# The score banks of a linear attention as one unit with fixed readers, and a one-column product ahead of its four products

## The chip, the cores and the metric

The kernel runs on one core of a Trainium2 chip. The metric is the device time of one execution in microseconds (us). For the kernel before there are three runs: 2646.0, 2646.59 and 2646.84 us, median 2646.59.

## The reference, cut to what matters

The reference is a stack of four transformer-like layers on an activation of 4 sequences of 1024 positions and 128 features, all fp32. Each layer normalises, runs an attention-like part, adds it with a gate, normalises again and runs a feed-forward part. The change lies in the attention part of the second layer ("layer 1"), which is itself a small transformer of 4 inner layers with 16 heads of 8 features and causal linear attention in chunks of 128 positions:

```python
KV = jnp.einsum('bnchd,bnche->bnhde', k, v)
KVcum = jnp.cumsum(KV, axis=1) - KV
inter = jnp.einsum('bnchd,bnhde->bnche', q, KVcum)
den_inter = jnp.einsum('bnchd,bnhd->bnch', q, Kcum)
scores = jnp.einsum('bnchd,bnkhd->bnhck', q, k)
mask = jnp.tril(jnp.ones((CHUNK, CHUNK), dtype=bool))
scores = jnp.where(mask, scores, 0.0)
intra = jnp.einsum('bnhck,bnkhe->bnche', scores, v)
out = (inter + intra) / (den_inter + den_intra + ATT_EPS)[..., None]
```

After each attention comes an output product, a layer norm, a feed-forward part with Gelu, and another layer norm. The change concerns `scores` and the causal mask on them.

## The kernel before, in words

The activation lies feature-major in SBUF, 128 partitions by 4 x 1024 columns. A *step* n (0 to 7) is one chunk of 128 positions of all four sequences, so 512 columns. Layer 1's attention (`l1_attn`) has 4 inner layers of 8 steps, 32 steps in all, and in each of them 4 *batches* b, one a sequence: 128 batches.

The order of the work is made in two places. The kernel has a planner of its own, `Flow`: each strand of the work is a generator that asks for buffers (`take`, `one`), tells the planner what it costs an engine (`run(PE=...)`), and marks what it has done. The planner picks the strand that can start first by its own clock, the lower rank first, and so fixes the order in which the program is written. Buffers are kept in stocks by kind; those that came free first are handed out first (`sort` by `free_at`). When the program is built, a scheduler below may still move single instructions of an engine past each other where their data allow it. On the chip each engine then works through its own queue in that order and waits on semaphores.

PSUM has eight banks. In this part three are for general use ("ps"), one holds the attention's numerator ("acc"), and four are for scores ("sp", line 850).

For each batch the strands do this:

- `scores` (lines 981 to 994) takes the four score banks and writes them by four products, d = 2, 3, 1, 0. Product d uses 32 of the 128 partitions (rows 32d to 32d+31 of TensorE's array): the keys of that row group as weights (32x128) and the queries of four heads as 512 columns. All products are recorded by the helper `mm` (line 291). An fp32 product shows as two records (two passes) in the trace.
- `mask_dve` (996 to 1008) multiplies the scores of d = 0, 1, 2 with the causal mask into SBUF tiles "at" on VectorE, line 1005.
- `mask_act` (1010 to 1023) copies the scores of d = 3 into SBUF on ScalarE (line 1018), and GpSimd multiplies them with the mask there (line 1021).
- `values` (1055 to 1086) multiplies the masked scores with the values (line 1080) into "acc", 16 small products a batch, 32 output rows each.

Around them, `prep` makes queries, keys, values and denominators of a step up to three steps ahead (Exp on ScalarE, line 895), `state` sums the running KV, `attn_out` closes a step, and `tail` runs the output norm and the feed-forward part (Gelu on ScalarE, line 1127) up to one step behind. Exp and Gelu lie in different function tables of ScalarE, so a change between them puts an ACT_TABLE_LOAD before the instruction.

In the kernel before, the four banks are four buffers of the stock "sp". Their order in the stock follows from when they came free, so the bank that ScalarE read for one batch becomes bank 0 of the next, and the banks of d = 0, 1, 2 become those of 1, 2, 3. In the built program VectorE masks d = 2 first, then 1, then 0.

Of the kernel before, what the change touches and what calls it, by code (L numbers as in the profile page):

```python
# [12 lines left out]
ALU = mybir.AluOpType  # L13
# [97 lines left out]
class Flow:  # L111
# [43 lines left out]
    def run(self, chains):  # L155
        live = [{"gen": g, "t": 0.0, "want": None, "rank": 0.0, "no": i} for i, g in enumerate(chains)]
        while live:
            ready, asked = [], set()
            for c in sorted(live, key=lambda c: (c["rank"], c["no"])):
                if c["want"] is not None and c["want"][0] == "take":  # L160
                    kind = c["want"][1][0]
                    if kind in asked:
                        continue
                    asked.add(kind)
                s = self._start(c)
                if s is not None:
                    ready.append((s, c))
            assert ready, [c["want"] for c in live]
            first = min(s for s, _ in ready)
            at, c = next((s, c) for s, c in ready if s <= first + self.SLACK)  # L170
            got = None
            if c["want"] is None or c["want"][0] == "rank":
                self.at = c["t"]
            elif c["want"][0] == "spawn":
                self.at = c["t"]
                live.append({"gen": c["want"][1], "t": c["t"], "want": None, "rank": c["rank"], "no": c["no"]})
            elif c["want"][0] == "run":
                end = c["t"]
                table, costs = c["want"][1]
                if table and table != self.table:  # L180
                    self.table = table
                    self.clock["ACT"] += self.TABLE
                for e, cost in costs.items():
                    self.clock[e] = max(self.clock[e], c["t"]) + cost
                    end = max(end, self.clock[e])
                c["t"] = self.at = end + self.LATENCY
            elif c["want"][0] == "wait":
                c["t"] = self.at = at
            else:
                kind, n = c["want"][1]  # L190
                self.free[kind].sort(key=lambda b: b.free_at)
                got = [self.free[kind].pop(0) for _ in range(n)]
                c["t"] = self.at = at
            try:
                c["want"] = c["gen"].send(got)
                if c["want"][0] == "rank":
                    c["rank"] = c["want"][1]
            except StopIteration:
                live.remove(c)
# [6 lines left out]
def take(kind, n=1):  # L206
    return ("take", (kind, n))


def one(kind):  # L210
    (b,) = yield take(kind)
    return b


def rank(r):

    return ("rank", r)
# [7 lines left out]
def wait(key):  # L225
    return ("wait", key)


def mm_len(n, m=P):

    return max(n, m) * 0.00167 + 0.01


def dve_len(n):
    return 0.16 + 0.00104 * n


def act_len(n):
    return 0.25 + 0.00083 * n


def pool_len(n):
    return 0.2 + 0.0021 * n
# [6 lines left out]
def adaln_stack_kernel(ctx: ExitStack, tc: tile.TileContext, a):  # L250
    nc = tc.nc
    V, S, G, PE = nc.vector, nc.scalar, nc.gpsimd, nc.tensor
# [37 lines left out]
    def mm(out, lhsT, rhs, start=True, stop=True):  # L290
        PE.matmul(out, lhsT, rhs, start=start, stop=stop)  # L291

    def rep(ap, n):

        return ap.unsqueeze(1).to_broadcast([ap.shape[0], n, ap.shape[1]])
# [5 lines left out]
    def v4(t):  # L301
        return t.rearrange("p (a b) -> p a b", b=P)
# [11 lines left out]
    def K(name):  # L314
        lo, hi = _CONST[name]
        return cst[:, lo:hi]
# [9 lines left out]
    ident, mu, sl = K("ident"), K("mu"), K("sl")  # L326
# [148 lines left out]
    def flow():  # L475
        return Flow()

    def banks():
        return [ps() for _ in range(6)] + [acc() for _ in range(2)]
# [4 lines left out]
    def norm_stock(fl, n):  # L484

        fl.stock("xt", [v4(norm_tile(("ln_xc", "ln_sq", "ln_xn")[i % 3])) for i in range(n)])
        for kind, shape in (("st", (P, 4, 6)), ("mv", (P, 4, 2)), ("ve", (P, 4)), ("rs", (P, 4))):
            stock(fl, kind, 2, shape)
# [352 lines left out]
    def l1_attn():  # L841
        y4 = h4
        fl = flow()
# [3 lines left out]
        psum = banks()  # L847
        fl.stock("ps", psum[:3])
        fl.stock("acc", psum[3:4])
        fl.stock("sp", psum[4:])  # L850
        norm_stock(fl, 3)
        fl.stock("z", [v4(norm_tile(tag)) for tag in ("ln_xc", "ln_sq", "ln_xn")])
        stock(fl, "qx", 2, (P, 4, B, P))
# [124 lines left out]
        ats, nums = {}, {}  # L978
        every = [(l, n) for l in range(L1L) for n in range(NS)]

        def scores():

            for l, n in every:
                yield rank(l * NS + n)
                yield wait(("prep", l, n))
                k, qx = ready[l, n][1].t, ready[l, n][5].t
                for b in range(B):
                    sps = yield take("sp", 4)
                    yield run(PE=mm_len(512) + 0.2)
                    for d in (2, 3, 1, 0):  # L990
                        g = slice(32 * d, 32 * d + 32)
                        mm(v4(sps[d].t), k[g, b, :], qx[g, :, b, :])
                    ats[l, n, b] = [sps, None, None]
                    fl.mark(("scores", l, n, b))

        def mask_dve():
            for l, n in every:
                yield rank(l * NS + n)
                for b in range(B):
                    yield wait(("scores", l, n, b))  # L1000
                    sps = ats[l, n, b][0]
                    at3 = yield take("at", 3)
                    yield run(DVE=3 * dve_len(512))
                    for d in range(3):
                        V.tensor_tensor(at3[d].t, v4(sps[d].t), rep(mu, 4), ALU.mult)  # L1005
                    fl.give(*sps[:3])
                    ats[l, n, b][1] = at3
                    fl.mark(("dve", l, n, b))

        def mask_act():  # L1010
            for l, n in every:
                yield rank(l * NS + n)
                for b in range(B):
                    yield wait(("scores", l, n, b))
                    sp = ats[l, n, b][0][3]
                    a = yield from one("at")
                    yield run(ACT=act_len(512))
                    S.copy(a.t, v4(sp.t))  # L1018
                    fl.give(sp)
                    yield run(POOL=pool_len(512))  # L1020
                    G.tensor_tensor(a.t, a.t, rep(mu, 4), ALU.mult)  # L1021
                    ats[l, n, b][2] = a
                    fl.mark(("act", l, n, b))
# [92 lines left out]
        def tail_step(l, n, z):  # L1116
# [22 lines left out]
            if l == L1L - 1:  # L1139
# [4 lines left out]
                fl.give(o)  # L1144

        chains = [attn_out(), state(), values(), mask_dve(), mask_act(), scores()]
        fl.run(chains + [tail(0), tail(1), prep(0), prep(1), first()])

# [699 lines left out]
    for i, half in enumerate([l0, l1_attn, l1_ffn, l2_attn, l2_ffn, l3_attn, l3_ffn]):  # L1848
        if half is l1_attn:
            early.close()  # L1850
        if half is l2_attn:
            late.close()
        with tc.tile_pool(name=f"half{i}", bufs=2) as wk:
            half()
# [99 lines left out]
```

## Time and profile before

One execution was profiled. It took 2641.42 us in all, with a span of 2639.7 us from its first to its last instruction, at a mean granted TensorE clock of 0.929.

| | us | share of the span |
|---|---|---|
| profiled execution | 2641.42 | |
| its span | 2639.7 | |
| TensorE busy | 2308.3 | 87% |
| TensorE weight loads | 1387.7 | 53% |
| VectorE busy | 1333.0 | 50% |
| ScalarE busy | 1154.9 | 44% |
| GpSimd busy | 892.2 | 34% |
| layer 1's attention, by its lines | about 370 to 1540 | 44% |

"PE" is TensorE's products, "PEld" its weight loads, which overlap them; DVE is VectorE, ACT ScalarE, POOL GpSimd. A group line names the line of the kernel, the engine, the operation, the tile written and the tiles read, then the number of records, the busy time in us (the union of the records), the mean of one in ns, and the engine's idle time just before them with what ended it. A line of the timeline has the start in us, how long the merged records lasted, the engine, the group and the number of records merged. A line of the windows view has the stretch and, for each engine, its busy time and number of records, then the clock and DMA figures.

### The profile page before, as it was taken

What the parts mean: (1) busy time and instruction counts of PE and PEld (TensorE: products, weight loads), DVE (VectorE), ACT (ScalarE), POOL (GpSimd) and SP (SyncE); (2) the same over time, 40 slices, a digit from 0 to 9 for tenths busy, and PEclk for the clock granted to TensorE, in tenths of its full rate; (3) what the DMA queues carried; (4) which work ended last, traced back from release to release, by engine and by line L of the source; (5) the groups of instructions that cost most, each with busy time, mean ns of one, the idle gap of its engine ahead of it and who ended that gap; (6) DMA issues with size and microseconds to landing.
All of it is one profiled execution on the core that took longest, in us unless ns stands there. A gap on an engine that the chain in (4) does not pass through costs nothing.

```text
span 2639.7 us, 36709 instructions
## 1 busy us (share of the span) xinstructions
PE 2308.3 (87%) x13822; PEld 1387.7 (53%) x13822; DVE 1333.0 (50%) x3930; ACT 1154.9 (44%) x1964; POOL 892.2 (34%) x885
## 2 busy tenths in 40 slices
PE   5999989899999988889899869999799878788966
PEld 4654445454545444444454434444789633687842
DVE  5764346664654556655665554343654224455422
ACT  3653245445545444444444333333544226545424
POOL 1334444332433333333333222333634001544400
PEclk9999989998999989999999888999899879899978
DMA  5323300000000000000000001110000000000001
GB/s 209 88 67 99 101 0 1 1 1 1 1 1 1 1 1 1 1 1 1 1 1 1 1 33 64 65 65 33 1 1 1 1 26 7 1 1 1 1 1 48
DMA packets 29010, 61.46 MB, mean 23 GB/s; under 512 B 4256, under 2 KB 4512, under 8 KB 27808
## 3 DMA queue, kind: packets, MB, share of 16 engines
q1 hardware_dynamic: 27072, 53.86, 6.3%
q0 software_dynamic: 896, 3.16, 0.4%
q8 instruction: 109, 1.79, 0.3%
q10 hardware_dynamic: 864, 2.09, 0.2%
q14 instruction: 69, 0.57, 0.1%
HBM read 56.74 MB, written 2.36 MB: 22 GB/s over the span
## 4 chain that ended last, share of the span: by engine, by line
PE 64%; DVE 17%; ACT 7%; POOL 6%; issue 3%; DMA 1%; SPq 0%; ACTq 0%; POOLq 0%; DVEq 0%
PE ps L291 38%; PE acc L291 15%; PE ps L1080 4%; POOL rs L515 2%; DVE at L1005 2%; DVE st L510 2%; PE ps L526 2%; PE ps L501 1%; DVE ln_sq L518 1%; POOL at L1021 1%; DVE ln_xc L518 1%; DVE ve L513 1%; PE ps L1258 1%; DVE x L455 1%; DVE ln_xn L518 1%
## 5 line engine op out<-in xcount | busy, mean ns | idle before, releaser
L291 PE MATMUL ps<-h,w 128*128 128x512 f32 x760 | 380.3, 616 | 33.3 <-DVE ln_xc L1104 8.7
L291 PEld LDWEIGHTS ps<-h,w 128*128 128x128 f32 x760 | 140.5, 197 | 191.1 <-issue 133.8
L1021 POOL TENSOR_TENSOR at<-at,cst 128x512 f32<-128x512 f32 x128 | 162.7, 1271 | 202.8 <-ACT at L1018 198.3
L291 PE MATMUL acc<-qx,k 32*128 32x512 f32 x512 | 209.7, 669 | 6.9 <-DVE at L1005 6.9
L291 PE MATMUL acc<-fu,w 128*128 128x512 f32 x432 | 210.6, 607 | 0.9 <-POOL fu L818 0.9
L515 POOL TENSOR_TENSOR rs<-ve,mhalf 128x4 f32<-128x4 f32 x120 | 122.9, 1024 | 252.6 <-DVE ve L513 230.1
L291 PE MATMUL ps<-qx,k 32*128 32x512 f32 x512 | 198.7, 671 | 7.2 <-DVE at L1005 7.2
L1080 PE MATMUL ps<-at,vz 128*32 128x128 f32 x4096 | 168.2, 292 | 36.8 <-POOL at L1021 30.7
L1235 POOL TENSOR_TENSOR lv<-cl,cst 128x512 f32<-128x512 f32 x112 | 141.2, 1273 | 164.0 <-PE ps L291 92.3
L1080 PEld LDWEIGHTS ps<-at,vz 128*32 128x32 f32 x4096 | 116.4, 116 | 111.7 <-issue 45.0
L1005 DVE TENSOR_TENSOR at<-acc,cst 128x512 f32<-128x512 f32 x190 | 126.9, 681 | 74.2 <-PE acc L291 46.1
L1005 DVE TENSOR_TENSOR at<-ps,cst 128x512 f32<-128x512 f32 x194 | 129.2, 680 | 56.6 <-PE acc L291 29.1
L1127 ACT ACTIVATE fu<-ps,cols 128x512 f32<-128x512 f32 x128 | 87.9, 687 | 156.3 <-PE ps L291 155.5
L818 POOL TENSOR_TENSOR fu<-fu,gate 128x512 f32<-128x512 f32 x88 | 110.9, 1266 | 131.0 <-DVE fu L814 114.9
L291 PE MATMUL ps<-fu,w 128*128 128x512 f32 x256 | 150.3, 672 | 5.3 <-ACT fu L1127 5.2
L291 PE MATMUL ps<-y,w 128*128 128x512 f32 x256 | 145.5, 652 | 8.5 <-DVE tmp L1040 2.1
L1203 ACT ACTIVATE fu<-ps,cols 128x512 f32<-128x512 f32 x128 | 88.0, 687 | 131.8 <-PE ps L291 128.5
L1207 POOL TENSOR_TENSOR fu<-fu,gate 128x512 f32<-128x512 f32 x64 | 83.4, 1310 | 166.7 <-ACT fu L1203 143.8
L291 PEld LDWEIGHTS acc<-fu,w 128*128 128x128 f32 x432 | 81.8, 195 | 95.2 <-issue 86.8
L1206 DVE TENSOR_TENSOR fu<-fu,gate 128x512 f32<-128x512 f32 x64 | 51.9, 823 | 119.7 <-ACT fu L1203 118.1
L291 PE MATMUL ps<-iU,lv 128*128 128x128 f32 x608 | 93.0, 301 | 20.4 <-DVE iU L1269 16.9
L291 PEld LDWEIGHTS ps<-iU,lv 128*128 128x128 f32 x608 | 83.2, 211 | 28.8 <-issue 12.1
(489 smaller groups left out, 4686.2 us busy)
## 6 DMA issues: line engine op xcount, KB each, us to landing
gate<-gd SPq DMA_DIRECT2D x96, 256.0 KB
w<-in_w SPq DMA_DIRECT2D x7, 1024.0 KB
gate<-gd SPq DMA_DIRECT2D x16, 224.0 KB
gate<-gd SPq DMA_DIRECT2D x16, 192.0 KB
gate<-gd SPq DMA_DIRECT2D x16, 160.0 KB
x<-in_x SPq DMA_DIRECT2D x8, 256.0 KB
gate<-gd SPq DMA_DIRECT2D x16, 128.0 KB
out_x<-x SPq DMA_DIRECT2D x8, 256.0 KB
```

Of the source, the lines that this page charges most:

```text
L291: PE.matmul(out, lhsT, rhs, start=start, stop=stop)
L510: V.bn_stats(st.t[:, t, :], xt[:, t, :])
L515: G.tensor_tensor(rs.t, ve.t, mhalf, ALU.pow)
L518: V.tensor_scalar(xt[:, t, :], xt[:, t, :], mv.t[:, t, 0:1], rs.t[:, t : t + 1], ALU.subtract, ALU.mult)
L818: G.tensor_tensor(u.t, u.t, g.t, ALU.mult)
L1005: V.tensor_tensor(at3[d].t, v4(sps[d].t), rep(mu, 4), ALU.mult)
L1021: G.tensor_tensor(a.t, a.t, rep(mu, 4), ALU.mult)
L1080: PE.matmul(num[g, b, :], vz[:, b, s * P + 32 * d : s * P + 32 * d + 32], at4[d].t[:, s, :], start=n == 0 and s == 0 and b == 0, stop=s == ...
L1127: S.activation(flat(u.t), pb.t, AF.Gelu, bias=C(f"l1_b1{l}", f))
L1203: S.activation(u.t, pa.t, AF.Relu, bias=C("l1f_b1", 2 * e + j))
L1207: G.tensor_tensor(us[1].t, us[1].t, g.t, ALU.mult)
L1235: G.tensor_tensor(b.t, cl.t, rep(lvl[:, k * P : (k + 1) * P], B), ALU.mult)
```

## The change

The four banks become one buffer of the stock, handed out and given back as a whole, so that d always has the same bank. The bank is given back by `through`, which VectorE's and ScalarE's strands both call and which frees it at the second call. Before the four products comes a one-column product into the first column of bank 3, with the same row group as d = 3; the d = 3 product then overwrites that column. The planner's cost of a batch rises from `mm_len(512) + 0.2` to `+ 0.3`.

```diff
-        fl.stock("sp", psum[4:])
+        fl.stock("sp", [psum[4:]])
...
-                    sps = yield take("sp", 4)
-                    yield run(PE=mm_len(512) + 0.2)
+                    quad = yield from one("sp")
+                    yield run(PE=mm_len(512) + 0.3)
+
+
+                    mm(v4(quad.t[3])[:, 0, 0:1], k[96:, b, :], qx[96:, 0, b, 0:1])
                     for d in (2, 3, 1, 0):
                         g = slice(32 * d, 32 * d + 32)
-                        mm(v4(sps[d].t), k[g, b, :], qx[g, :, b, :])
-                    ats[l, n, b] = [sps, None, None]
+                        mm(v4(quad.t[d]), k[g, b, :], qx[g, :, b, :])
+                    ats[l, n, b] = [quad, None, None]
                     fl.mark(("scores", l, n, b))
+
+        def through(quad):
+
+            if half_read.pop(quad, None) is None:
+                half_read[quad] = fl.at
+                return
+            fl.give(quad)
+
+        half_read = {}
...
-                    sps = ats[l, n, b][0]
+                    quad = ats[l, n, b][0]
                     at3 = yield take("at", 3)
                     yield run(DVE=3 * dve_len(512))
                     for d in range(3):
-                        V.tensor_tensor(at3[d].t, v4(sps[d].t), rep(mu, 4), ALU.mult)
-                    fl.give(*sps[:3])
+                        V.tensor_tensor(at3[d].t, v4(quad.t[d]), rep(mu, 4), ALU.mult)
+                    through(quad)
...
-                    sp = ats[l, n, b][0][3]
+                    quad = ats[l, n, b][0]
                     a = yield from one("at")
                     yield run(ACT=act_len(512))
-                    S.copy(a.t, v4(sp.t))
-                    fl.give(sp)
+                    S.copy(a.t, v4(quad.t[3]))
+                    through(quad)
```

## The prediction

> **What bounds the kernel now.** I read the page first, then the windows over layer 1's attention (370 to 1540 us by the first and last of its lines), the groups in that stretch by form, the waits of TensorE, and last the timeline around single batches of scores.
>
> ```profile
> span 2639.7 us, 36709 instructions
> ...
> PE 2308.3 (87%) x13822; PEld 1387.7 (53%) x13822; DVE 1333.0 (50%) x3930; ACT 1154.9 (44%) x1964; POOL 892.2 (34%) x885
> ...
> L291 PE MATMUL acc<-qx,k 32*128 32x512 f32 x512 | 209.7, 669 | 6.9 <-DVE at L1005 6.9
> ...
> L291 PE MATMUL ps<-qx,k 32*128 32x512 f32 x512 | 198.7, 671 | 7.2 <-DVE at L1005 7.2
> ```
>
> The two last lines are the products of the change: 1024 records, two passes for each of 512 fp32 products. TensorE is the busiest engine, and in the stretch that the change touches it is busier still, with every other engine at 59% or less:
>
> ```profile
> 370.00:1540.00 1170.00, 1052.70 (x7909) 562.66 (x7907) 685.34 (x1834) 545.35 (x820) 401.98 (x452) 0.94 0.00 1
> ```
>
> The columns are PE, PEld, DVE, ACT and POOL. PE is busy for 1052.7 of 1170 us, so a microsecond of TensorE there is nearly a microsecond of time; only 117 us are idle, and 14.1 of them wait on the DVE masks in front of scores. The same window, for the scores' tile alone, gives 259.2 us of PE. If the four products of each of the 128 batches always ran side by side, it would be about 128 x 1.06 = 136 us. The timeline shows why it is more:
>
> ```profile
> 824.00 0.70 PE L291 MATMUL acc<-qx,k 32*128 32x512 f32 x2
> 824.01 0.70 PE L291 MATMUL ps<-qx,k 32*128 32x512 f32 x2
> 824.53 0.59 PE L291 MATMUL acc<-qx,k 32*128 32x512 f32 x2
> 824.54 0.59 PE L291 MATMUL ps<-qx,k 32*128 32x512 f32 x2
> 825.07 1.13 PE L291 MATMUL ps<-y,w 128*128 128x512 f32 x2
> ```
>
> Four products (eight records) hold TensorE from 824.00 to 825.07, 1.07 us. And one product alone:
>
> ```profile
> 838.53 1.06 PE L291 MATMUL ps<-cst,tmp 128*128 128x16 f32 x8
> 839.53 1.12 PE L291 MATMUL acc<-qx,k 32*128 32x512 f32 x2
> ```
>
> It takes 1.12 us, and elsewhere the next product starts 1.05 us after such a single one (612.25 to 613.30). So the cost is per *run* of adjacent score products, not per product. I grouped the timeline of the whole stretch into such runs: 212 of them, with 71 of one product and 58 of four; the median from a run's start to the next instruction is 1.05 us for one product and 1.07 us for four. The order of the built program has 212 runs too (76 of one, 30 of two, 48 of three, 58 of four).
>
> **What the skill says.** "TensorE: Matmul & The Clock Gate", Part 3 (packing small matmuls), says that products in different groups of 32 rows run at the same time. The trace agrees: eight records in 1.07 us. Its section on LDWEIGHTS says that a 32x128 weight load costs as much as a 128x128 one, since the columns count. The trace agrees: 190 ns mean for the scores' loads, 195 to 200 ns for the full ones of y,w and fu,w. "TensorEngine Tiling (Array Packing)", Instruction Overhead, says that a product with one free column takes as long as one with 60; the trace of before has no such product. "ScalarE: Activation LUTs", What ACT_TABLE_LOAD costs, gives 1283 ns and a drain of 1380 ns besides. The trace has the 1283 ns exactly, and no drain that I can see (the ACTIVATE starts some 20 ns after the load).
>
> **The change part by part.**
>
> *Fixed banks.* Before, the ACT's bank of one batch becomes bank 0 of the next, so the product that waits for ACT is the last of the four and the first waits for DVE's second mask. After, the first product (d=2) reuses the bank that DVE masks first, d=1 the second and d=0 the third. Where TensorE comes early, the last product starts after DVE's third mask in both, so the end of such a stall doesn't move. This part I cost at nothing: the quad was only taken when all four banks were free before as well, and its cover is the other TensorE work that the order puts in front; if that were gone, a batch would be spread over DVE's masks of 681 ns each, as one already is at 429.85 (3.08 us idle and then 2.5 us for four products). That is paid before and after.
>
> *Order.* The scheduler lays the instructions anew. Counted in the order of both built programs, without the one-column products, the score runs fall from 212 to 193, and one of these is a double quad: 194 turns. Runs of four rise from 58 to 75 (and the double), threes fall from 48 to 31, singles from 76 to 61. So 18 turns less at 1.06 us: **-19.1 us** of TensorE, on the path, since the stretch is bound there. The runs of the value products (158 in both) do not change, and the instruction counts of every other group stay. No DMA is added or moved.
>
> *One-column product.* 128 new ones, two passes each. In 125 places score products follow directly, and 3 stand alone. Each needs its own load of 128 weight columns in row group 96 to 127, and the true d=3 product needs that group again, with its weights loaded once more. The bounds: from above, the 16-column products, which are bound by their loads: eight records between 838.53 and 839.53 are 0.125 us a pass, 0.25 us a product, so 128 x 0.25 = 32 us. From below: 60 columns at the rate of a 512-column pass (0.53 us) are 0.062 us, twice 0.12 us (an estimate from the tiling page and the trace); and part of that can lie beside d=2, which is in another row group, so down to 0.05 us, 6 us in all. Below nothing is excluded, since an instruction more takes TensorE time and what it does for the order is counted above. I take 0.20 us, nearer the upper end, because the weight load of the following d=3 in the same group cannot lie beside this one: 128 x 0.20 = **+25.6 us**, also on the path.
>
> *Its wait.* The product takes over the wait for ACT (57 of 128 carry one). Behind it on TensorE stands all else, the value products of earlier batches and the next layer's chunks too. ACT's copy is 0.585 us against DVE's 3 x 0.681 = 2.04 us, so it is rarely the later. Nothing for the wait itself.
>
> *ACT's order.* The new plan (0.3 us for a batch in place of 0.2) alternates Exp and Gelu more: the built order has 94 table loads at these two lines in place of 72.
>
> ```profile
> L895 ACT ACT_TABLE_LOAD x36 | 46.2, 1283 | 0.6
> L1127 ACT ACT_TABLE_LOAD x36 | 46.2, 1283 | 0.6
> ```
>
> 22 more at 1.283 us are 28.2 us of ACT, which is busy for only 545 of 1170 us. How much reaches TensorE? TensorE's idle time that ACT ended sums to about 20 us in the stretch (fu 5.2, kt 3.6, k and q 5.5, the rest), and POOL's mask behind ACT's copy ended 30.7 us more. If all of that were due to the 72 loads it would be 0.7 us a load and 22 more would cost 15; if none, 0. I take 5 us: **+5 us**.
>
> Sum: -19.1 + 25.6 + 5 = +11.5 us. The profiled execution took 2641.4 us (2639.7 of span and 1.7 around it), which gives 2652.9. It lies 5.2 us under the median of the three runs, 2646.6; on that median it is 2658.
>
> **Rivals.** About 0.2%, 5.3 us, is what a measurement of this kernel can tell from no change.
>
> *The one-column product is hidden* and the fuller quads count: the other side. The mechanism is its 0.05 us in row group 96 to 127 beside d=2; then -19.1 + 6.4 and no cost on ACT is -12.7, 2634 us. For it: row groups do run side by side, and weight loads are pulled ahead. Against it: the same row group is needed twice in a row. It decides if the product costs under 0.11 us (19.1 less 5.3, over 128).
>
> *Gain and price cancel:* at about 0.15 us a product (19.2 us) with ACT's loads hidden, 2647 us. For it: ACT is idle for half of the stretch. It is also where I land if the built order doesn't decide, since the scheduler's idea of what is ready isn't the chip's, and stalls take the place of splits.
>
> *ACT becomes the late one:* each new load delays a chain that TensorE waits for, 28.2 us in full. Then -19.1 + 25.6 + 28.2 = +34.7, 2681 us. For it: POOL's mask waits 198 us for ACT's copy. Against it: those waits are mostly themselves waits for TensorE.
>
> **How the numbers follow.** The forecast, 2652 to 2668 us, has 0.45; the hidden product, faster, 0.27; cancellation, within 0.2%, 0.20; ACT, slower, 0.08. So faster 0.27, same 0.20, slower 0.53. The range from 2633 to 2672 takes in the bounds of the small product and leaves out most of the ACT case and what lies below the hidden one. As cases of both signs hold most of the chance: the likeliest one's own range is 2652 to 2668.
>
> **What would show it.** In the profile after: a group of 256 records with one column, and in the timeline the start of d=3 some 0.2 us after it; if all four start within 0.1 us of it, the hidden case holds. PE over the scores' tile: about 259 - 19 + 26 = 266 us if I am right, under 250 if hidden. Score runs by time: 194 turns. Table loads at the Exp and Gelu lines: 94, and TensorE's idle time ended by ACT about 5 us longer. The prediction fails if the stretch's idle time (117 us) moves by more than some 15 us either way, which the new order can do through waits that I have not costed.

## The result and the profile after

The kernel after takes 2625.5 us (median of four runs, 2621.0 to 2628.0) against 2646.3 us before; the ratio is 0.9922, 95% interval 0.9905 to 0.9939. So it is 20.8 us faster, where I had forecast 11.5 us slower, and the time lies below my range.

The profiled execution has a span of 2623.1 us, 16.6 us under that of before. These are the page's lines that answer to those of before:

```profile
span 2623.1 us, 37170 instructions
...
PE 2300.8 (88%) x14078; PEld 1400.8 (53%) x14078; DVE 1325.5 (51%) x3930; ACT 1183.0 (45%) x1986; POOL 891.1 (34%) x885
```

TensorE has 256 records more and is all the same 7.5 us less busy; ScalarE is 28.1 us busier, which is the 22 table loads. TensorE's instructions after layer 1's attention stand in the same order as before, so the cause is to be looked for in that part. Its last output (the gated add into x at line 455) starts at 1541.7 us instead of 1552.2, so the part gives 10.5 of the 16.6 us; the rest of the kernel, from there to the end, takes 1081.4 us against 1087.5, and over all profiles of this study it scatters between 1079 and 1091. By form, over 370 to 1540 us, the groups of the scores and the table loads are (busy us, mean ns, then idle before and its releaser):

```profile
L291 PE MATMUL acc<-qx,k 32*128 32x512 f32 x512 | 213.9, 652 | 1.4 <-DVE at L1017 1.4
L291 PE MATMUL ps<-qx,k 32*128 32x512 f32 x512 | 170.1, 659 | 0.3 <-DVE at L1017 0.2
...
L895 ACT ACT_TABLE_LOAD x47 | 60.3, 1283 | 0.8
L1139 ACT ACT_TABLE_LOAD x47 | 60.3, 1283 | 0.8
L291 PE MATMUL acc<-qx,k 32*128 32x1 f32 x256 | 49.6, 261 | 5.8 <-POOL k L898 4.0 <-ACT at L1030 1.6
```

The idle time in front of the scores on VectorE's masks was 14.1 us before and is 1.7 now. The part as a whole, from 370 us to its end, in the windows view; PE, PEld, DVE, ACT and POOL again. First the kernel before, then after:

```profile
370.00:1552.20 1182.20, 1056.12 (x7921) 564.83 (x7919) 690.50 (x1861) 547.49 (x823) 403.99 (x454) 0.93 0.00 1
```

```profile
370.00:1541.70 1171.70, 1058.18 (x8178) 586.61 (x8176) 680.03 (x1861) 576.51 (x845) 402.76 (x454) 0.93 0.00 1
```

TensorE's busy time rises by 2.1 us, and its idle time (length less busy) falls from 126.1 to 113.5 us. The whole gain of the part is idle time, a term that my sum had left where it was, plus 5 us for ScalarE's table loads.

The same for the scores' tile, after: 262.0 us, against 259.2 before, where I had said 266. That this is near is luck, as the experiments will show: the two terms behind it, -19.1 and +25.6, measure about -5 and +8 in this tile.

```profile
370.00:1541.70 1171.70, 262.04 (x1280) 87.94 (x1280) 85.67 (x128) 0.93 0.00 1
```

The timeline of one batch with its one-column product (merged with the group acc<-qx,k, so its form shows first):

```profile
453.27 0.70 PE L291 MATMUL acc<-qx,k 32*128 32x1 f32 x2
453.29 0.70 PE L291 MATMUL ps<-qx,k 32*128 32x512 f32 x2
453.40 1.00 PE L291 MATMUL acc<-qx,k 32*128 32x1 f32 x3
453.82 0.59 PE L291 MATMUL ps<-qx,k 32*128 32x512 f32 x2
454.03 0.59 PE L291 MATMUL acc<-qx,k 32*128 32x512 f32 x1
454.54 0.86 PE L1092 MATMUL ps<-at,vz 128*32 128x128 f32 x24
```

Three of the four products run their second pass from about 453.82 on, and that of d = 3, the one in the row group of the small product, from 454.03. The next instruction starts 1.27 us after the batch's first, where it was 1.07 before. Over the 74 runs of ten records the median is 1.28 us. So in an undivided batch the product does cost 0.21 us of TensorE, as I had taken it for all 128 (0.20). Where the order divides a batch, so that only d = 2 stands behind the small product (38 runs), the next instruction starts by the median 1.06 us after the run's first, where one product alone takes 1.05. Still the kernel is faster.

### The profile page after: what moved, and what is told of

Same layout as the page of the kernel before. It is cut to its first block, busy times and chain, and to the rows that moved or that the text cites. A ratio compares the mean times of both kernels' runs of the same rounds, so it can differ in the third digit from the quotient of the medians.

```text
span 2623.1 us, 37170 instructions
## 1 busy us (share of the span) xinstructions
PE 2300.8 (88%) x14078; PEld 1400.8 (53%) x14078; DVE 1325.5 (51%) x3930; ACT 1183.0 (45%) x1986; POOL 891.1 (34%) x885
## 4 chain that ended last, share of the span: by engine, by line
PE 65%; DVE 16%; ACT 8%; POOL 6%; issue 3%; DMA 2%; SPq 0%; ACTq 0%; POOLq 0%; DVEq 0%
PE ps L291 37%; PE acc L291 16%; PE ps L1092 4%; POOL rs L515 3%; PE ps L526 2%; DVE st L510 2%; DVE at L1017 1%; PE ps L501 1%; DVE ln_sq L518 1%; DVE ln_xc L518 1%; ACT L895 1%; DVE x L455 1%; PE ps L1270 1%; POOL at L1033 1%; DVE ln_xn L518 1%
## 5 line engine op out<-in xcount | busy, mean ns | idle before, releaser
L291 PE MATMUL acc<-qx,k 32*128 32x512 f32 (+1 forms) x768 | 218.0, 522 | 7.2 <-POOL k L898 4.0
L1092 PE MATMUL ps<-at,vz 128*32 128x128 f32 x4096 | 163.2, 287 | 28.3 <-POOL at L1033 23.5
L1017 DVE TENSOR_TENSOR at<-ps,cst 128x512 f32<-128x512 f32 x256 | 166.5, 682 | 39.5 <-PE ps L291 35.1
L291 PE MATMUL ps<-qx,k 32*128 32x512 f32 x512 | 170.1, 659 | 0.3 <-DVE at L1017 0.2
L1030 ACT COPY at<-acc 128x512 f32<-128x512 f32 x128 | 74.5, 582 | 162.3 <-PE acc L291 108.5
L1017 DVE TENSOR_TENSOR at<-acc,cst 128x512 f32<-128x512 f32 x128 | 87.6, 684 | 91.2 <-PE ps L291 61.0
L291 PEld LDWEIGHTS acc<-qx,k 32*128 32x128 f32 x768 | 73.0, 189 | 68.2 <-issue 49.0
```

What stands on the lines that cost most here:

```text
L1017: V.tensor_tensor(at3[d].t, v4(quad.t[d]), rep(mu, 4), ALU.mult)
L1030: S.copy(a.t, v4(quad.t[3]))
L1092: PE.matmul(num[g, b, :], vz[:, b, s * P + 32 * d : s * P + 32 * d + 32], at4[d].t[:, s, :], start=n == 0 and s == 0 and b == 0, stop=s == ...
```

## The experiments

The change holds four things: the banks are *fixed*; the unit's *free time* on the planner's clock is another; the *one-column product* is new; the *planner's cost* goes from 0.2 to 0.3. The second I had not seen. Each ratio below is to the kernel before, run on the same chip beside it, with its 95% interval. A ratio of 0.001 is 2.6 us.

**First: the product, the cost, and the two kinds of bank.** The profile left five theories: A, the gain comes from the banks and the order, and the product is a cost; B, the product makes the gain; C, the product only fills waits; F, the fixed banks make it; P, a lucky order of the planner.

Without the product:

```diff
-                    mm(v4(quad.t[3])[:, 0, 0:1], k[96:, b, :], qx[96:, 0, b, 0:1])
```

> The kernel after without its one-column products; the rest as it is (fixed banks as a unit, planner's cost 0.3). Its order has 196 score runs, near the 193 of after. In after's profile a run of four with its one-column product goes on after 1.28 us, one without after 1.07, so the products cost some 0.21 us x 128 = 27 us of TensorE. Theory A (the gain comes from the fixed banks and the order, and the one-column product is a cost): about 2625 - 27 = 2598 us. Theory B (the one-column product, which takes over the wait for ACT, makes the gain): back to about 2646 us or above. Theory C (it works as padding that other waits would fill anyway): 2615 to 2630 us.

Measured: 2617.2 us, 0.9907 (0.9891 to 0.9923), 0.0015 under after, or 4 us, with intervals that overlap. B falls, and C's range holds. A's size is wrong: instead of 27 us the product gives back 4 us. In the scores' tile it is 7.6 us (254.4 us without it, 262.0 with it), since it costs its 0.21 us only where d = 3 stands behind it in the same run.

The kernel before with the cost alone:

```diff
-                    yield run(PE=mm_len(512) + 0.2)
+                    yield run(PE=mm_len(512) + 0.3)
```

> The kernel before with only the planner's cost of a batch raised from 0.2 to 0.3. Its order has 200 score runs in place of 212 and 132 table loads in place of 118. Theory P (the gain is a luckier order of the planner, whatever moved it): about 2625 to 2635 us. Theory F (fixed banks make it): 2640 to 2655 us.

Measured: 2667.8 us, 1.0097 (1.0082 to 1.0111). This is above both ranges. The cost makes the kernel slower, though its score runs are 12 fewer. So it is no part of the gain.

The kernel before with the cost and the product:

```diff
+                    mm(v4(sps[3].t)[:, 0, 0:1], k[96:, b, :], qx[96:, 0, b, 0:1])
                     for d in (2, 3, 1, 0):
```

> The kernel before with the cost 0.3 and the one-column product ahead of the four, into the bank that d = 3 is about to write; the banks still rotate. Its order is that of the cost alone (200 score runs, 132 table loads) but for the 128 new products. Theory A: some 27 us above the run with the cost alone. Theory B: below that run.

Measured: 2671.2 us, 1.0108 (1.0092 to 1.0125), 3 us over the cost alone, which can't be told from none. Neither A's 27 us nor B holds.

The kernel after with the old cost:

```diff
-                    yield run(PE=mm_len(512) + 0.3)
+                    yield run(PE=mm_len(512) + 0.2)
```

> The kernel after with the planner's cost put back to 0.2, fixed banks and one-column product kept: 195 score runs, 142 table loads. Theory F (the fixed banks make the gain): 2620 to 2632 us. Theory P (the cost's effect on the plan makes it): 2640 us or above.

Measured: 2595.5 us, 0.9821 (0.9808 to 0.9834), 27 us faster than after and below F's range. No theory had this. It means that what the unit brings is about twice the net gain, and the cost takes half of it back. But its score runs (195) are nearly those of after (193), so runs don't explain it.

**Second: the banks or the plan.** In `through` the unit is given back by whichever strand the *program's order* has second, and at that strand's time. ScalarE's copy of one bank ends earlier on the planner's clock than VectorE's three masks. The two times were written out while the kernel after was built: in 62 of 128 batches the second caller's time is the earlier one, in 45 of them by 1.40 to 1.44 us and in the rest by less. So in half of the batches the planner believes the banks free up to 1.4 us before VectorE is through. On the chip the semaphores still hold each product back until its bank is read, so only the order changes. If the later of the two times is taken, the built order is, instruction by instruction, that of the old planner with sorted banks. Below, *true* free time means the later of the two, as before the change (the old plan), and *early* free time means what `through` gives (the new plan).

Old plan, fixed banks:

```diff
-                    sps = yield take("sp", 4)
+                    sps = sorted((yield take("sp", 4)), key=lambda buf: place[id(buf)])
```

> The kernel before (four buffers, cost 0.2, no one-column product), where the four banks are sorted after they are taken, so that d always has the same bank. The built order differs from that of before in some 20 places an engine, and is the same, instruction by instruction, as that of a unit whose free time is set to the later of its two readers. Theory F (the fixed banks shorten the waits on the chip): 2595 to 2620 us. Theory E (the unit is freed too early on the planner's clock: in 62 of 128 batches the strand that gives it back last in the program's order ends 1.4 us before VectorE's; this moves the plan, and the banks themselves do nothing): 2638 to 2648 us.

Measured: 2627.4 us, 0.9933 (0.9919 to 0.9947). Above theory F's range and below theory E's: something comes with this kernel under the old plan, but not the 55 us that the new plan shows below. Its order on TensorE is not quite that of before, so it isn't the banks alone.

New plan (early free time, cost 0.2, no product), rotating banks:

```diff
                     quad = yield from one("sp")
+                    quad.t = [quad.t[i] for i in (3, 0, 1, 2)]
```

> The unit of after at cost 0.2 without the one-column product, but with the four banks of the unit rotated at every batch as before. TensorE's order is that of the next kernel, instruction by instruction. Theory F: about 2640 us. Theory E: the same as the next kernel within 5 us, about 2585 to 2600.

Measured: 2591.5 us, 0.9804 (0.9786 to 0.9823).

The same with fixed banks (the unit without the product, at cost 0.2):

```diff
-                    yield run(PE=mm_len(512) + 0.3)
-                    mm(v4(quad.t[3])[:, 0, 0:1], k[96:, b, :], qx[96:, 0, b, 0:1])
+                    yield run(PE=mm_len(512) + 0.2)
```

> The unit of after at cost 0.2, fixed banks, no one-column product. From the runs so far (fixed unit with the product at 0.2: 2595; the product's removal at 0.3: -8): 2585 to 2595 us on all theories that let the three parts add.

Measured: 2590.9 us, 0.9790 (0.9777 to 0.9802). With TensorE's order equal, fixed and rotating banks differ by 0.0014 with overlapping intervals. Theory E holds here: under the new plan the fixed readers do nothing that can be measured. These two are the fastest kernels of the study, 55 us under before and 35 us under after.

The unit always freed at its earlier reader's time:

```diff
+            quad.free_at = min(first, fl.at)
```

> As the kernel before this one, but the unit's free time on the planner's clock is always the earlier of its two readers', not only where the program's order has ACT's strand second (62 of 128). 188 score runs, 136 table loads. Theory E in its strong form (an earlier free time makes TensorE take scores earlier, which is good): at or below the unit at cost 0.2, 2580 to 2595 us. Theory L (any new plan is a draw of some +-25 us around before's time, and this one was a lucky draw): anywhere from 2600 to 2670 us.

Measured: 2620.1 us, 0.9901 (0.9887 to 0.9915). Still faster than before, but 29 us over the mixed case. So the strong form of E falls: earlier is not always better.

**Third: cause or draw.** The planner's order reacts to any small change, so one lucky plan would look like this too. Four more plans, two from each family; only the cost and the free time differ (`max` for the true time):

```diff
-                    yield run(PE=mm_len(512) + 0.2)
+                    yield run(PE=mm_len(512) + 0.15)
...
+            quad.free_at = max(first, fl.at)
```

> Unit with the early free time, fixed banks, no one-column product, planner's cost 0.15 (195 score runs, as at 0.2). Theory E (an early free time is good in itself, the cost shifts little): 2585 to 2620 us. Theory L (each plan is a draw): anything from 2590 to 2670, no nearer to its family than to the other.

Measured: 2598.6 us, 0.9822 (0.9806 to 0.9839).

> The same at cost 0.25: 181 score runs, the fewest of all. By score runs alone (1.06 us each, 14 fewer than at 0.2) it would be 15 us under 2591, so 2576 us. Theory E: 2585 to 2620. Theory L: 2590 to 2670.

Measured: 2595.2 us, 0.9817 (0.9795 to 0.9838). It has 14 score runs fewer than at 0.2 and isn't faster.

> Unit with the true free time (the later of the two readers), fixed banks, no one-column product, cost 0.15: 218 score runs. Theory E: 2625 to 2670 us, like the others with the true time (2627 at 0.2). By score runs alone 4 more than at 0.2: 2631. Theory L: 2590 to 2670.

Measured: 2636.0 us, 0.9970 (0.9958 to 0.9983).

> The same at cost 0.25: 210 score runs. Theory E: 2625 to 2670 us; by score runs alone 2623; theory L: 2590 to 2670.

Measured: 2641.3 us, 0.9989 (0.9976 to 1.0002).

At 0.15 the early time is better by 0.0148, at 0.2 by 0.0143, at 0.25 by 0.0172. That is no scatter of draws: each early plan beats each true one, by 38 to 45 us at equal cost. Nor is it the clock: over their runs the three true kernels have mean granted clocks of 0.935 to 0.939, the three early ones of 0.931 to 0.933.

**Fourth: a dose, and what was left.** A fixed amount is taken off the true free time:

```diff
+            quad.free_at = max(first, fl.at) - 0.7
```

> Unit, fixed banks, no one-column product, cost 0.2, free time = the later reader's less 0.7 us in every batch. Theory E: the gain comes with the dose: between 2591 (the change's mixed early time) and 2627 (true time), or as low as 2591. Theory M (only the mixed case was a lucky plan): 2625 or above.

Measured: 2600.2 us, 0.9827 (0.9811 to 0.9843).

```diff
+            quad.free_at = max(first, fl.at) - 1.4
```

> The same with 1.4 us taken off in every batch; ACT's time lies 1.4 us before VectorE's, so this is near to the earliest-reader kernel (2620). Theory E: 2590 to 2620. Theory M: 2625 or above.

Measured: 2610.4 us, 0.9866 (0.9849 to 0.9882). Both hold with E, against the theory of one lucky plan. From no dose to 0.7 to 1.4 us the times are 2627, 2600 and 2610: of the three the middle one is best.

True free time and fixed banks at cost 0.3 (as above with `max` and 0.3):

> Unit with the true free time, fixed banks, no one-column product, cost 0.3. TensorE's order is that of the rotating kernel with the cost alone (2668 us), instruction by instruction. If fixed banks save 19 us under an old-type plan: 2649. If they do nothing: 2668.

Measured: 2663.5 us, 1.0070 (1.0053 to 1.0086), against 1.0097 (1.0082 to 1.0111) with rotating banks and the same order on TensorE. So here, with TensorE's order equal, fixed banks give at most some 7 us, not 19. And this is a fourth pair for the free time: the unit at cost 0.3 without the product, with early time, had 0.9907, which is 43 us less at equal cost.

The kernel before with the product alone:

```diff
+                    mm(v4(sps[3].t)[:, 0, 0:1], k[96:, b, :], qx[96:, 0, b, 0:1])
                     for d in (2, 3, 1, 0):
```

> The kernel before with the one-column product added and nothing else (rotating banks, cost 0.2, 210 score runs). If the product costs what it did under the other plans (3 to 8 us): 2648 to 2652 us. If its full 0.22 us x 128 = 28 us lands on the path: 2672.

Measured: 2628.2 us, 0.9928 (0.9912 to 0.9945): 18 us *faster* than before, with an order on TensorE that differs from it in 6 places and 128 products more. Neither value that I had written down holds, and no run takes the 18 us apart further.

**Fifth: both under the old plan, and before once more.** The product added to the old plan with fixed banks (`max`, cost 0.2):

> The change as it stands but with the unit's true free time and cost 0.2: fixed banks and one-column product under the old plan (212 score runs, 118 table loads). If fixed banks (-19) and the product (-18) each cure a wait of their own: 2609 us. If both only move before out of an unlucky state of the clock or of one wait: 2625 to 2632. If the product costs what it does under the new plan: 2632 to 2636.

Measured: 2631.1 us, 0.9954 (0.9940 to 0.9969). This is in the second range: the two gains of 18 us don't add up; together they make 12. Against the early time with the product at the same cost (0.9821) it is a fifth pair, 35 us.

Before with an empty last line:

> The kernel before, unchanged but for an empty last line. Time 2646 us. If its granted clock belongs to it: 0.929 +- 0.002, against 0.936 and 0.934 of the two near copies. If the clock is that of one execution: anywhere from 0.925 to 0.936.

Measured: 2642.9 us, 1.0003 (0.9996 to 1.0009), and a granted clock of 0.926 in its profile, after 0.929 in the first one. Its 20 runs lie between 0.926 and 0.932. The near copies have 0.936 (fixed banks), 0.934 (product) and 0.936 (both) in their profiles, and means of 0.936 to 0.937 over their runs. So the clock belongs to the kernel and not to one execution. These are the lines of the clocks, the first profile of before, then the near copy with fixed banks:

```profile
core 0: 2639.7 us, clock 0.929
```

```profile
core 0: 2627.2 us, clock 0.936
```

A clock higher by 0.007 to 0.010 of 0.93, on 2308 us of TensorE, would be 17 to 25 us (an estimate from these lines), as much as these kernels gain. So the old-plan gains go with a higher granted clock, and also with less idle time of TensorE in the part: 122.1, 115.3 and 114.8 us against 126.1. Which of the two makes them isn't shown, and the two are hardly apart. In the part, before's trace has the clock either full or half, with 25 stretches of half clock, each of 3.4 us or a multiple of it. 20 of them come behind 3.4 us in which TensorE stood idle for over 1 us, though after 30 more such pauses the clock stayed full. One of them:

```profile
1010.90:1014.30 3.40, 1.52 (x18) 0.77 (x22) 2.44 (x6) 0.07 (x1) 0.56 (x1) 0.99 0.02 5
1014.30:1017.70 3.40, 3.40 (x29) 1.88 (x21) 0.39 (x1) 2.60 (x3) 0.27 (x1) 0.50 0.00 0
1017.70:1021.10 3.40, 3.40 (x18) 1.40 (x17) 1.86 (x3) 2.15 (x4) 1.09 (x2) 1.00 0.00 0
```

TensorE is busy for 1.52 of 3.40 us, the next 3.40 us run at half clock, and then it is full again. The near copies have 21 to 23 such stretches. Why the few moved products save some of them was not found. A high clock alone doesn't make a fast kernel either: the true time at cost 0.15 has 0.940 in its profile, with TensorE 17.7 us less busy in the part than before, but idle for 13.2 us more, and gains 8 us.

## Why the prediction was wrong

**The step that failed** is "Fixed banks. ... This part I cost at nothing", with its ground that "the quad was only taken when all four banks were free before as well". That is true of the chip and not of the planner. In the sum it stands as the idle time of TensorE, which I left in place but for +5 us and which fell by 12.6 us in the part. The free time by which the planner decides had become, in 62 of 128 batches, that of the earlier reader, and this alone is worth 35 to 45 us at equal cost, in five pairs. I had read the order of the built program and taken from it the runs of scores and the table loads, but put the new order down to the cost of 0.3 alone. The cost alone, run by itself, makes the kernel 26 us slower, where I had +5 us for ScalarE and -19.1 us for the score runs.

**The way from before to after**, one step after the other, each measured (ratio, and the step in us at 2645 us a unit):

| kernel | ratio | step, us |
|---|---|---|
| before | 1 | |
| fixed banks, true free time, 0.2 | 0.9933 | -18 |
| early free time | 0.9790 | -38 |
| one-column product | 0.9821 | +8 |
| planner's cost 0.3 (after) | 0.9922 | +27 |

The steps depend on their order. With the cost first, the way is +26 (cost), -7 (fixed banks), -43 (early time) and +4 (product). The fixed banks are -18 under the old plan at 0.2, where the clock rises with them, and between -7 and +7 in the other three comparisons; the product is -19 on the old rotating plan, +3 to +8 in the other four. The early time (-35 to -45) and the cost (+26 to +48) held in all five comparisons of each.

**Where the time went** is seen in TensorE's waits over layer 1's attention, the longest first. Before:

```profile
PE ps L1080 <- POOL at L1021: 30.7, 26, 2.1
PE ps L291 <- DVE ln_xc L1104: 8.7, 5, 2.5
PE ps L291 <- DVE ln_xn L1104: 8.7, 4, 2.5
PE ps L291 <- DVE ln_sq L1104: 8.2, 4, 2.5
PE ps L291 <- DVE at L1005: 7.2, 7, 3.8
...
PE ps L1080 <- DVE at L1005: 5.6, 11, 1.5
```

The unit at cost 0.2, with early free time, the fastest kernel (lines 1091 and 1032 are the value products and GpSimd's mask):

```profile
PE ps L291 <- ACT fu L1138: 15.9, 16, 4.2
PE ps L1091 <- DVE at L1016: 11.9, 17, 2.6
PE ps L1091 <- POOL at L1032: 10.2, 12, 2.9
PE ps L1077 <- DVE tmp L1107: 6.6, 4, 2.7
```

The value products wait for GpSimd's mask, which stands behind ScalarE's copy (0.585 us and then 1.27 us). That wait is 30.7 us before, and 25 to 43 us in all kernels with the true time; at costs up to 0.25 it is 8 to 15 us in all with the early time. A plan that takes the next scores earlier would have their masks ready earlier; this reason is argued, not shown. Part of it comes back as a wait for VectorE's masks, 5.6 us before and 11.9 here. The wait on the VectorE step that closes the attention (line 1104 before, 25.6 us in the three lines above) falls to 1.8 us, while that on the step ahead of it (line 1107 here) rises from 2.0 to 6.6. In return TensorE waits longer for ScalarE: all waits that ACT ended sum to 21 us before, 33 us after and 40 us here. In after that is 12 us more, under my bound of 15 and over the 5 us that I took; that the table loads make it isn't shown apart from the rest of the plan. All in all idle time falls from 126.1 to 100.6 us in this kernel. And the busy time falls, from 1056.1 to 1038.1 us, of which the scores' tile gives 11 us, 248.2 us against 259.2 before. The part as a whole, and the scores' tile:

```profile
370.00:1508.70 1138.70, 1038.11 (x7923) 562.87 (x7921) 686.71 (x1862) 577.70 (x847) 403.25 (x454) 0.94 0.00 1
...
370.00:1508.70 1138.70, 248.21 (x1024) 70.54 (x1024) 86.62 (x128) 0.94 0.00 1
```

With rotating banks and the same order it is 241.3 us, 17.9 less than before for 17 runs fewer, which is the price of 1.05 us a run.

At cost 0.3 the mask's wait stands at 23.5 us (after) and 22.8 (without the product), so most of that benefit is gone again. Yet the early time gains as much there. So the mask's wait is one way in which it gains, and not the only one. This is the part at cost 0.3 without the product, first with true time, then with early time:

```profile
370.00:1575.60 1205.60, 1076.91 (x7923) 570.79 (x7921) 683.01 (x1861) 565.79 (x837) 404.23 (x454) 0.93 0.00 1
```

```profile
370.00:1537.80 1167.80, 1046.42 (x7923) 569.49 (x7921) 680.20 (x1861) 576.08 (x845) 402.93 (x454) 0.93 0.00 1
```

Here the busy time of TensorE falls by 30.5 us and the idle time by only 7.3. The value products alone give 19.6 of the 30.5: with true time at this cost they stand in 175 separate runs, with early time in 158, as before the change. That is also a good part of what the cost of 0.3 does to the kernel before: its value products rise from 158 to 175 runs and from 168.2 to 179.9 us. The prediction had counted these runs, but only in before and after, where they are equal.

**The other terms.** *Order*: 18 turns at 1.06 us, -19.1. The price held in one kernel (-17.9 for 17 runs, above), but not in the change itself: without the product it has 196 runs, 16 fewer than before, and 254.4 us in the scores' tile, only 4.8 less. And runs don't rank the kernels: the 181 runs at cost 0.25 give 2595 us, 195 runs at 0.2 give 2591, and 200 runs in the old plan at 0.3 give 2668. *One-column product*: 0.21 us of TensorE in undivided batches, as taken, but next to nothing where only d = 2 follows. In the scores' tile it is 7.6 us in the change and 14.0 us at cost 0.2 (262.2 against 248.2), and on the path it is 4 and 8 us and not 25.6. In both pairs the idle time falls by 8 us (to 113.5 and to 92.5): a good part of the product stands where TensorE would have waited. So the rule that "a microsecond of TensorE there is nearly a microsecond of time" was wrong for work placed just in front of a wait. *Its wait*: nothing, as said: 1.6 us of idle time on ScalarE's copy. *Rivals*: the faster side had 0.27, for the wrong reason: it put the gain down to fuller quads and a hidden product. The product is hidden in 38 runs and not in the 74 undivided batches.

The range failed because it had no width for the idle time. The last sentence of the prediction named a move of 15 us as the sign of being wrong; 12.6 us in the part was enough, since nothing in the sum allowed for it.

**What stays open**: why 0.7 us of early time is better than 1.4; why the cost of 0.3 does so much harm in both families, beyond the divided value products in the one and the returned mask's wait in the other; and what in near copies of before raises the granted clock.

## What to carry to other kernels

Where a planner written by hand decides the order, the times at which it believes buffers free are part of the kernel: compare them before and after a change, not only the instructions and their costs. On an engine that is 90% busy an added instruction need not be paid in full: where it stands in front of a wait, part of it fills the wait, and the remaining idle time may move more than everything that was counted. Take a change of several parts apart before keeping it: here the unit at the old cost without the new product is 35 us faster than the change as it stands.

## What the runs showed of the hardware

A product of one column, two passes, in a row group that a product close behind it needs, delays that product by 0.21 us (a second pass at 454.03 in place of 453.82), while the three in other row groups go ahead. In the same batch the four weight loads of that row group start 0.11 us apart (453.27, 453.38, 453.49 and 453.60), those of different row groups within 0.03 us. Where the batch was divided behind d = 2, the small product cost 0.01 us or less (1.06 us in place of 1.05). The granted clock of TensorE in layer 1's attention fell to half mostly behind 3.4 us with over 1 us of idle time, so a pause there can cost more than its own length. And kernels of nearly the same order had steady granted clocks of their own: 0.926 and 0.929 for before in two profiles, 0.934 to 0.936 for three near copies, with 12 to 19 us of time between them.
